# Output projection with channels on the partitions, its layer norm by products of ones, and c_fc_2 as a product of TensorE

## The chip, the cores and the metric

The kernel runs on one core of one Trainium2 chip. The metric is the device time of one execution in microseconds. The document speaks of the engines by the names that the profile gives them: PE (TensorE, the matrix products), PEld (its weight loads), DVE (VectorE), ACT (ScalarE), POOL (GpSimd), and SP, whose queue issues nearly all DMAs.

## The reference

Two layers work on an input of 4 batches, 384 channels and 32 x 32 positions. Layer 0 is a selective scan in four directions followed by a mixture of four experts; layer 1 is attention followed by a feed-forward part whose two weights are Kronecker products. The change touches only the end of layer 1, cut here to what matters:

```python
out = jnp.einsum('bhnm,bhmd->bhnd', attn, w)             # attention, 8 heads of 64
out = jnp.einsum('bne,ce->bnc', out, w_out) + b_out      # projection out, 512 -> 384
x = x + out                                              # residual
t = _to_tokens(x)
h = _ln_t(t) @ jnp.kron(c_fc_1, c_fc_2).T                # c_fc_1 (1536, 32), c_fc_2 (1, 12)
t = t + jax.nn.gelu(h, approximate=False) @ jnp.kron(c_proj_1, c_proj_2).T
x = _from_tokens(t, x)
```

`_ln_t` subtracts the mean over the 384 channels and divides by the root of the variance plus 1e-5. Because c_fc_2 has one row of 12, a token's 384 channels are first folded into 32 numbers (12 channels each, weighted by c_fc_2), called z below, and only these 32 go through c_fc_1.

## The kernel before, in words

A batch has 1,024 positions, worked on as two halves of 512 (`halves(i)`) or eight tiles of 128 (`MB`). The 384 channels are three chunks of 128 (`DC`).

The program has two strands. The scan strand (`scan_layer`) goes through batches 0 to 3 in turn. Its inner step, in `chunk`, multiplies on POOL (L438, and L466 for half of the tiles), makes decay factors on ACT (L447), scans and multiplies on DVE (L452, L459) and adds up on PE with a product of 512 columns (L473). There are 1,536 of these products, each shown as two PE instructions; one of them is called a row of the scan here. POOL's results lie in six buffers named bx, which the products of L473 free. The scan's loads (dtr, bcs) are issued by the SP queue.

The tail strand (`tail_batch`) does the rest of a batch: routing of its tokens to experts (`route`, whose DVE part is `places` and whose 16 scatters are issued by POOL at L681), the experts (L925, L940), their combination (L977), attention (L1026 to L1103) and `last_layers`. The tails of batches 0, 1 and 2 run beside the scan of later batches as far as they fit; routing of batch b+1 stands between the attention and the last layers of batch b. The tail of batch 3 comes after the whole scan.

No order is written out by hand. A scheduler merges the two strands into one fixed order of instructions for each engine while the program is built, by priorities and by its own estimate of times; on the chip each engine works through its own order, and an instruction that waits holds up those behind it. `last_layers` is issued with a raised priority. Tiles come from pools: a tile of tag "k4" takes any of 5 buffers for the batches 0 to 2 and of 4 for batch 3, and waits until the former user of a buffer is done. Attention weights (ex), the token tiles of routing and several small tiles of `last_layers` share this tag. Products in PSUM take one of 3 banks of tag "p" for batches 0 to 2, and of 6 for batch 3.

`last_layers` before the change, step by step:

- L1119 to L1123 load weights: wa and wb hold w_out (wb also c_fc_2 and b_out repeated over the partitions), wc the rest. L1129 scales a part of wc on DVE.
- L1135 loads the residual, one tile xt of 1.5 MB with tokens on the partitions. L1136 adds b_out to it on POOL.
- For each of the eight tiles of 128 tokens, L1142 makes the projection o_ps (tokens x 384 channels) from four pieces of attention output. DVE adds it to xt (L1145), multiplies the sum with c_fc_2 back into the bank (L1146) and adds up twelves into zt (L1147); `stats` takes mean and variance of each token (L541, L542).
- L1153 to L1157 finish the layer norm on the 32 numbers of z instead of on 384 channels and write them four times side by side; L1164 turns them by PE, and L1168 copies them out of PSUM.
- `hidden` makes the 1,536 hidden values of one half in two sets of six chunks: products (L1180), copies (L1186), one gelu over six (L1189), then f_acc (L1197).
- For each chunk of output channels L1207 multiplies with pj2 in four pieces, and L1211 adds xt turned by a product with the identity. ACT copies the result out (L1216), and SP stores it (L1217).

Of the kernel before, what the change touches and what calls it, by code (L numbers as in the profile page):

```python
# [17 lines left out]
P = 128  # L18
B = 4
D = 384  # L20
DC = D // P
HW = 32
L = HW * HW
HF = 512
NH = L // HF
# [26 lines left out]
MB = L // P  # L52
# [6 lines left out]
KR = 32  # L59
KJ = D // KR  # L60
# [7 lines left out]
    ("lnb", DC),  # L68
    ("pj2", KJ),
    ("c2", KJ),  # L70
]
COL = {}
_at = 0
# [37 lines left out]
def halves(i):  # L111
    return slice(i * HF, (i + 1) * HF)


class Body:
    def __init__(self, ctx, tc, a):
        self.tc, self.nc, self.a = tc, tc.nc, a
        nc = self.nc
        const = ctx.enter_context(tc.tile_pool(name="const", bufs=1))
        self.const = const  # L120


# [16 lines left out]
        self.c2sum = const.tile([P, 1], F32, tag="c2sum", name="c2sum")  # L139
        lo, hi = COL["c2"]  # L140
        nc.vector.tensor_reduce(self.c2sum, self.cols[:, lo:hi], AX.X, ALU.add)

    def exp_again(self, ins):

# [963 lines left out]
    def last_layers(self, b, att, room):  # L1108

        nc, a = self.nc, self.a
        nq = P // KR
        nt = INNER // P


        wa = room.tile([P, nt - 1, D], "kw", "wa")
        nc.sync.dma_start(out=wa, in_=a["wa"].rearrange("p (t d) -> p t d", d=D))  # L1119
        wb = room.tile([P, 3, D], "kw", "wb")  # L1120
        nc.sync.dma_start(out=wb, in_=a["wb"].rearrange("p (t d) -> p t d", d=D))
        wc = room.tile([P, 3, D], "kw", "wc")
        nc.sync.dma_start(out=wc, in_=a["wc"].rearrange("p (t d) -> p t d", d=D))  # L1123
        c2, bout = wb[:, 1, :], wb[:, 2, :]
        fc1 = wc[:, 0, :].rearrange("p (q m) -> p q m", m=P)
        pj1 = wc[:, 1, :].rearrange("p (f r) -> p f r", r=KR)
        pj2 = wc[:, 2, :]
        lo, hi = COL["pj2"]
        nc.vector.tensor_mul(  # L1129
            pj2.rearrange("p (r j) -> p r j", j=KJ), pj2.rearrange("p (r j) -> p r j", j=KJ),  # L1130
            self.cols[:, lo:hi].unsqueeze(1).to_broadcast([P, KR, KJ]),
        )

        xt = room.tile([P, MB, D], "k12", "xt")
        nc.sync.dma_start(out=xt, in_=self.tokens(b))  # L1135
        nc.gpsimd.tensor_add(xt, xt, bout.unsqueeze(1).to_broadcast([P, MB, D]))  # L1136
        zt = room.tile([P, MB, KR], "zt", "zt")
        for m in range(MB):
            ps = room.bank("p", "o_ps")[:, :D]
            for t in range(nt):  # L1140
                w = wa[:, t, :] if t < nt - 1 else wb[:, 0, :]
                nc.tensor.matmul(  # L1142
                    ps, att[t][:, m * P : (m + 1) * P], w, start=(t == 0), stop=(t == nt - 1)
                )
            nc.vector.tensor_add(xt[:, m, :], xt[:, m, :], ps)  # L1145
            nc.vector.tensor_mul(ps, xt[:, m, :], c2)  # L1146
            nc.vector.tensor_reduce(  # L1147
                zt[:, m, :], ps.rearrange("p (r j) -> p r j", j=KJ), AX.X, ALU.add
            )

        mean, rstd = self.stats(xt, self.eps5, room)
        shift = room.tile([P, MB], "shift", "shift")
        nc.vector.tensor_scalar(shift, mean, self.c2sum, None, op0=ALU.mult)  # L1153
        nc.vector.tensor_sub(zt, zt, shift.unsqueeze(2).to_broadcast([P, MB, KR]))
        z4 = room.tile([P, MB, nq, KR], "k4", "z4")
        for r in range(nq):
            nc.vector.tensor_mul(  # L1157
                z4[:, :, r, :], zt, rstd.unsqueeze(2).to_broadcast([P, MB, KR])
            )
        z = room.tile([P, L], "k4", "z")  # L1160
        for i in range(NH):
            ps = room.bank("p", "z_ps")
            for j in range(HF // P):
                nc.tensor.transpose(  # L1164
                    ps[:, j * P : (j + 1) * P],
                    z4[:, i * (HF // P) + j].rearrange("p r k -> p (r k)"), self.ident,
                )
            nc.vector.tensor_copy(z[:, halves(i)], ps)  # L1168


        ng = 6

        def hidden(i, at):
            hs = room.tile([P, ng, HF], "k12", "hs")
            early = None
            for f in range(at, at + ng, 2):
                banks = [room.bank("p", "h_ps") for _ in range(2)]
                for o, ps in enumerate(banks):
                    rows = slice((f + o) % nq * KR, ((f + o) % nq + 1) * KR)
                    ins = nc.tensor.matmul(  # L1180
                        ps, fc1[rows, (f + o) // nq, :], z[rows, halves(i)], start=True, stop=True
                    ).ins
                    if o == 0 and early is not None:
                        self.depend(ins, early)
                done = [
                    nc.scalar.copy(hs[:, f - at + o, :], ps).ins for o, ps in enumerate(banks)  # L1186
                ]
                early = done[0]
            self.exp_again(nc.scalar.activation(hs, hs, AF.Gelu).ins)  # L1189
            return hs  # L1190

        for i in range(NH):
            out = room.bank("o", "f_acc")
            for at in range(0, FC, ng):
                hs = hidden(i, at)
                for f in range(at, at + ng):
                    nc.tensor.matmul(  # L1197
                        out[f % nq * KR : (f % nq + 1) * KR, :], pj1[:, f, :], hs[:, f - at, :],
                        start=(f < nq), stop=(f >= FC - nq),
                    )  # L1200
            y = room.tile([P, HF], "k4", "fy")
            nc.vector.tensor_copy(y, out)
            for c in range(DC):
                ps = room.bank("p", "fo_ps")
                for j in range(HF // P):
                    cols = slice(j * P, (j + 1) * P)
                    nc.tensor.matmul(  # L1207
                        ps[:, cols], pj2[:, c * P : (c + 1) * P], y[:, cols],
                        start=True, stop=False,
                    )  # L1210
                    nc.tensor.matmul(  # L1211
                        ps[:, cols], xt[:, i * (HF // P) + j, c * P : (c + 1) * P], self.ident,
                        start=False, stop=True,
                    )
# [159 lines left out]
def layouts(inputs):  # L1374

    i = {k: np.asarray(v) for k, v in inputs.items()}

    def vec(v, lead):
        return np.moveaxis(v.reshape(*lead, P, -1), len(lead), 0).reshape(P, -1)
# [8 lines left out]
        "lnb": vec(i["L0_conv_ln_bias"], (DC,)),  # L1388
        "pj2": np.broadcast_to(i["L1_ffn_c_proj_2"].reshape(1, -1), (P, KJ)),
        "c2": np.broadcast_to(i["L1_ffn_c_fc_2"].reshape(1, -1), (P, KJ)),  # L1390
    }
# [3 lines left out]
    fc1 = i["L1_ffn_c_fc_1"].T  # L1395
    wx = np.zeros((D, KG // 2, XP), np.float32)
    wdt = np.zeros((KG, XP, D), np.float32)
    for k in range(KG):
# [19 lines left out]
        "wqkv": i["L1_conv_w_qkv"].T,  # L1418
        "wa": wout[:-1].transpose(1, 0, 2).reshape(P, -1),
        "wb": np.concatenate(  # L1420
            [
                wout[-1],
                np.broadcast_to(np.tile(i["L1_ffn_c_fc_2"].reshape(-1), KR), (P, D)),
                np.broadcast_to(i["L1_conv_b_out"], (P, D)),
            ],
            axis=1,
        ),
        "wc": np.concatenate(
# [25 lines left out]
```

## Time and profile before

| | |
|---|---|
| median of 3 runs | 4369.77 us (4367.19 to 4371.41) |
| the profiled execution | 4344.16 us |
| its span, from first to last instruction | 4342.4 us |
| mean granted clock of PE | 0.857 |
| busy: PE, DVE, ACT, POOL | 3303.7, 2915.6, 2504.3, 3049.3 us |
| last L438 of the scan begins | about 3480 us |
| o_ps (L1142) runs, batches 0 to 3 | about 1735 to 1780, 2745 to 2795, 3710 to 3780, 4232 to 4254 us |

The table of busy time counts how long an engine worked in a stretch; the list of waits says which instruction stood idle for which other one; a row of the groups gives line, engine, operation, output and inputs, shapes and count, then total busy time, the mean of one in ns, and the idle time before them with what ended it. The profiled execution is one execution of its own; it was 25 us shorter than the median of the three timed runs.

### The profile page before, as it was taken

To read this page: it belongs to the slowest core of one execution; us is meant where nothing else is said; L and a number is where in the kernel's file an instruction comes from. 1 tells how busy PE (TensorE), PEld (TensorE's weight loads), DVE (VectorE), ACT (ScalarE), POOL (GpSimd) and SP (SyncE) were. 2 spreads that over 40 slices of the span, in tenths; PEclk is the share of its full clock that TensorE was granted. 3 is DMA by queue.
4 is the path that set the end of the run, shared out by engine and by line. 5 is a ranking of instruction groups with operands and counts; after the bars stand their busy time and mean duration, and the time that the engine had idled before them with its cause. 6 is when DMAs were issued, how large, how long until landed. Compare 5 with 4: busy or idle time off the path is not lost. (4 is left out here: it accounts for less than half of the span.)

```text
span 4342.4 us, 45822 instructions
## 1 busy us (share of the span) xinstructions
PE 3303.7 (76%) x13340; PEld 1577.5 (36%) x13340; DVE 2915.6 (67%) x4331; ACT 2504.3 (58%) x4460; POOL 3049.3 (70%) x1475
## 2 busy tenths in 40 slices
PE   6444454398987885679986887569987889998896
PEld 2111111155552222245553222235554235666323
DVE  5999997887787868878886778967877730200101
ACT  5555555466665775467665776466665664343353
POOL 5999997798888968789998688778988820000100
PEclk8666666599998996789998999779998899999897
DMA  5444564567795535458888434457789443335200
GB/s 142 129 119 127 142 160 120 180 196 233 220 281 151 151 118 147 145 161 241 228 242 246 137 107 124 136 149 223 214 237 268 121 147 107 116 127 210 64 17 16
DMA packets 410131, 694.49 MB, mean 160 GB/s; under 512 B 50832, under 2 KB 209424, under 8 KB 409872
## 3 DMA queue, kind: packets, MB, share of 16 engines
q1 hardware_dynamic: 400560, 665.07, 53.6%
q0 software_dynamic: 8192, 25.17, 1.8%
q8 instruction: 107, 1.75, 0.2%
q14 instruction: 152, 1.25, 0.1%
q10 hardware_dynamic: 1120, 1.24, 0.1%
HBM read 569.79 MB, written 121.50 MB: 159 GB/s over the span
## 5 line engine op out<-in xcount | busy, mean ns | idle before, releaser
L438 POOL TENSOR_TENSOR bx<-dtr,bcs 128x1024 f32<-128x1024 f32 x768 | 1795.1, 2364 | 216.2 <-PE acc L473 103.2
L447 ACT ACTIVATE da<-dtr,nega 128x512 f32<-128x512 f32 x1536 | 1045.2, 690 | 994.2 <-DVE bx L459 628.9
L466 POOL TENSOR_TENSOR bx<-bx,bcs 128x1024 f32<-128x1024 f32 x384 | 905.2, 2362 | 160.3 <-DVE carry L463 67.3
L473 PE MATMUL acc<-bx,sel 128*32 128x512 f32 x3072 | 499.2, 702 | 342.4 <-POOL bx L466 273.7
L925 PE MATMUL h_ps<-xc,w 128*128 128x256 f32 (+1 forms) x3168 | 659.5, 363 | 52.0 <-DMA w<-in_w 27.0
L940 PE MATMUL y_ps<-w,hs 128*128 128x384 f32 x1824 | 649.6, 509 | 57.5 <-ACT hs L933 43.6
L925 PEld LDWEIGHTS h_ps<-xc,w 128*128 128x128 f32 x3168 | 547.6, 196 | 219.9 <-issue 92.3
L452 DVE TENSOR_TENSOR_SCAN bx<-da,carry,bx 128x512 f32<-128x512 f32 x384 | 474.0, 1269 | 140.4 <-POOL bx L438 79.5
L452 DVE TENSOR_TENSOR_SCAN bx<-da,bx 128x512 f32<-128x512 f32 x384 | 453.2, 1210 | 107.7 <-ACT da L447 61.7
L452 DVE TENSOR_TENSOR_SCAN da<-da,carry,bx 128x512 f32<-128x512 f32 x384 | 476.9, 1274 | 62.7 <-ACT da L447 51.8
L459 DVE TENSOR_TENSOR bx<-da,bcs 128x512 f32<-128x512 f32 x768 | 509.5, 679 | 3.1
L452 DVE TENSOR_TENSOR_SCAN da<-da,bx 128x512 f32<-128x512 f32 x384 | 455.7, 1219 | 76.0 <-ACT da L447 54.9
L940 PEld LDWEIGHTS y_ps<-w,hs 128*128 128x128 f32 x1824 | 353.6, 198 | 346.0 <-issue 75.7
L1055 ACT ACTIVATE ex<-s_ps 128x512 f32<-128x512 f32 x512 | 300.1, 590 | 157.1 <-PE s_ps L1049 156.1
L1049 PE MATMUL s_ps<-w 64*128 64x512 f32 x1024 | 309.9, 666 | 54.5 <-ACT ex L1055 53.8
L1095 PE MATMUL o_acc<-ex,vt 128*64 128x512 f32 x1024 | 285.6, 637 | 32.9 <-ACT ex L1055 23.5
L473 PEld LDWEIGHTS acc<-bx,sel 128*32 128x32 f32 x3072 | 77.0, 116 | 640.9 <-POOL bx L466 386.6
L930 ACT ACTIVATE hs<-h_ps,bb 128x256 f32<-128x256 f32 (+1 forms) x528 | 199.9, 439 | 185.3 <-PE h_ps L925 180.6
L961 POOL TENSOR_TENSOR diag<-ident,g_weight 128x1024 f32<-128x1024 f32 x8 | 15.1, 1899 | 326.9 <-DMA w<-in_w 312.1
L944 DVE TENSOR_TENSOR y<-y_ps,bb 128x384 f32<-128x384 f32 x76 | 41.7, 549 | 259.0 <-PE y_ps L940 259.0
L363 PE MATMUL dt_ps<-xd,wdt 108*128 108x512 f32 x192 | 123.9, 732 | 73.3 <-ACT mag L402 43.9
L1049 PEld LDWEIGHTS s_ps<-w 64*128 64x128 f32 x1024 | 83.5, 192 | 254.2 <-ACT ex L1055 202.3
(214 smaller groups left out, 3688.4 us busy)
## 6 DMA issues: line engine op xcount, KB each, us to landing
w<-in_w SPq DMA_DIRECT2D x352, 576.0 KB
dtr<-dd SPq DMA_DIRECT2D x1536, 128.0 KB
bcs<-both SPq DMA_DIRECT2D x512, 128.0 KB
dd<-one_e SPq DMA_DIRECT2D x96, 256.0 KB
dd<-mag SPq DMA_DIRECT2D x96, 256.0 KB
rows<-zero SPq DMA_DIRECT2D x76, 192.0 KB
xs<-rows SPq DMA_DIRECT2D x32, 384.0 KB
made<-y SPq DMA_DIRECT2D x32, 384.0 KB
```

The costliest lines, as they stand in the source:

```text
L438: pool = nc.gpsimd.tensor_mul(bx, dtr[q][1], bc[:, 0].unsqueeze(1).to_broadcast([P, 2, HF])).ins
L447: nc.scalar.activation(da, dtr[q][0][:, j, :], AF.Exp, scale=nega[:, col : col + 1])
L452: nc.vector.tensor_tensor_scan(run(h), run(da), run(bx[:, j, :]), 0.0 if first else hold, ALU.mult, ALU.add,)
L459: dve = nc.vector.tensor_mul(bx[:, j, :], h, cg).ins
L466: pool = nc.gpsimd.tensor_mul(bx, bx, cg.unsqueeze(1).to_broadcast([P, 2, HF])).ins
L473: nc.tensor.matmul(acc[lo : lo + DB, :], sel, out[q][:, j, :], start=(g == 0), stop=(g == NG - 1),)
L925: nc.tensor.matmul(ps[:, r, :], w1[(f + r) // wf][:, c, (f + r) % wf * P : ((f + r) % wf + 1) * P], xc[:, c, :], start=(c == 0), stop=(c = ...
L930: nc.scalar.activation(hs[:, f + r, :], ps[:, r, :], AF.Identity, bias=bb[:, f + r : f + r + 1])
L940: nc.tensor.matmul(out[:, :D], hs[:, f, t * P : (t + 1) * P], w2[f // wf][:, f % wf, :], start=(f == 0), stop=(f == FC - 1),)
L1049: ins = nc.tensor.matmul(ps, w[rows, j * P : (j + 1) * P], w[rows, halves(i)], start=True, stop=True).ins
L1055: done.append(nc.scalar.activation(ex[:, o, :], ps, AF.Exp, scale=HD**-0.5, accum_out=sums[:, t, 2 * j + o, i : i + 1],).ins)
L1095: ins = nc.tensor.matmul(out[cols, :], made[t][1][:, j, cols], ex[:, o, :], start=(j == 0), stop=(j == MB - 1),).ins
```

## The change

The projection is now made with channels on the partitions. For each half, three chunks of o_ps take four pieces of attention output, 512 columns wide; the residual is added in the same bank by products of its token tiles with the identity. It comes in four loads of two token tiles each (tag k4) in place of one. ACT evicts each chunk with b_out as a bias into x2 (channels x positions). Mean and variance come from products with a matrix of ones, as the earlier layer norms of this kernel do it; the centred values and their squares are needed only for the variance. z is a product of x2 with a matrix wz that holds c_fc_2, less its mean over the 384 channels (so that the mean of a token drops out); DVE subtracts that mean from wz once per batch. The inverse root is two activations over 512 columns, and z is its product with zp. At the output, one product of 512 columns stands for the four pieces, and DVE adds x2 while it copies out of PSUM, where ACT had copied. The rest of `last_layers` and all other functions are as they were; c2sum becomes c2mean.

```diff
-        wb = room.tile([P, 3, D], "kw", "wb")
+        wb = room.tile([P, 2, D], "kw", "wb")
...
-        c2, bout = wb[:, 1, :], wb[:, 2, :]
+        wz = wb[:, 1, :]
+        nc.vector.tensor_scalar(wz, wz, self.c2mean, None, op0=ALU.subtract)
...
-        xt = room.tile([P, MB, D], "k12", "xt")
-        nc.sync.dma_start(out=xt, in_=self.tokens(b))
-        nc.gpsimd.tensor_add(xt, xt, bout.unsqueeze(1).to_broadcast([P, MB, D]))
-        zt = room.tile([P, MB, KR], "zt", "zt")
-        for m in range(MB):
-            ps = room.bank("p", "o_ps")[:, :D]
-            for t in range(nt):
-                w = wa[:, t, :] if t < nt - 1 else wb[:, 0, :]
+        x2 = room.tile([P, DC, L], "k12", "x2")
+        zs = []
+        for i in range(NH):
+            part = []
+            for m in range(i * (HF // P), (i + 1) * (HF // P), 2):
+                part.append(room.tile([P, 2, D], "k4", "xt"))
+                nc.sync.dma_start(out=part[-1], in_=self.tokens(b)[:, m : m + 2, :])
+            for c in range(DC):
+                ps = room.bank("p", "o_ps")
+                chunk = slice(c * P, (c + 1) * P)
+                for t in range(nt):
+                    w = wa[:, t, chunk] if t < nt - 1 else wb[:, 0, chunk]
+                    nc.tensor.matmul(ps, w, att[t][:, halves(i)], start=(t == 0), stop=False)
+                for j in range(HF // P):
+                    nc.tensor.matmul(
+                        ps[:, j * P : (j + 1) * P], part[j // 2][:, j % 2, chunk], self.ident,
+                        start=False, stop=(j == HF // P - 1),
+                    )
+                nc.scalar.activation(
+                    x2[:, c, halves(i)], ps, AF.Identity, bias=self.col("bout", c)
+                )
+            mean = room.bank("p", "x2_mean")
+            for c in range(DC):
                 nc.tensor.matmul(
-                    ps, att[t][:, m * P : (m + 1) * P], w, start=(t == 0), stop=(t == nt - 1)
+                    mean, self.ones, x2[:, c, halves(i)], start=(c == 0), stop=(c == DC - 1)
                 )
-            nc.vector.tensor_add(xt[:, m, :], xt[:, m, :], ps)
-            nc.vector.tensor_mul(ps, xt[:, m, :], c2)
-            nc.vector.tensor_reduce(
-                zt[:, m, :], ps.rearrange("p (r j) -> p r j", j=KJ), AX.X, ALU.add
-            )
-
-        mean, rstd = self.stats(xt, self.eps5, room)
...
+            sq = room.tile([P, DC, HF], "k12", "x2_sq")
+            for c in range(DC):
+                nc.vector.scalar_tensor_tensor(
+                    sq[:, c, :], mean, -1.0 / D, x2[:, c, halves(i)], op0=ALU.mult, op1=ALU.add
                 )
-            nc.vector.tensor_copy(z[:, halves(i)], ps)
+                nc.scalar.activation(sq[:, c, :], sq[:, c, :], AF.Square)
+            zp = room.bank("p", "z_ps")
+            for c in range(DC):
+                nc.tensor.matmul(
+                    zp, wz[:, c * P : (c + 1) * P], x2[:, c, halves(i)],
+                    start=(c == 0), stop=(c == DC - 1),
+                )
+            var = room.bank("p", "x2_var")
+            for c in range(DC):
+                nc.tensor.matmul(var, self.ones, sq[:, c, :], start=(c == 0), stop=(c == DC - 1))
+            z = room.tile([P, HF], "k4", "z")
+            self.inverse_root(z, var, self.eps5, scale=1.0 / D)
+            nc.vector.tensor_mul(z, z, zp)
+            zs.append(z)
...
-                for j in range(HF // P):
-                    cols = slice(j * P, (j + 1) * P)
-                    nc.tensor.matmul(
-                        ps[:, cols], pj2[:, c * P : (c + 1) * P], y[:, cols],
-                        start=True, stop=False,
-                    )
-                    nc.tensor.matmul(
-                        ps[:, cols], xt[:, i * (HF // P) + j, c * P : (c + 1) * P], self.ident,
-                        start=False, stop=True,
-                    )
+                nc.tensor.matmul(ps, pj2[:, c * P : (c + 1) * P], y, start=True, stop=True)
                 o = room.tile([P, HF], "k4", "out")
-                nc.scalar.copy(o, ps)
+                nc.vector.tensor_add(o, ps, x2[:, c, halves(i)])
```

The weights that the host lays out follow: wb holds wz in place of the repeated c_fc_2 and b_out, and b_out joins the small columns.

More of the change, by code (lines that the diff above doesn't have):

```diff
@@ L70 @@
     ("c2", KJ),
+    ("bout", DC),
 ]
@@ L137, in __init__ @@
         nc.gpsimd.memset(self.minus1, -1.0)
-        self.c2sum = const.tile([P, 1], F32, tag="c2sum", name="c2sum")
+        self.c2mean = const.tile([P, 1], F32, tag="c2mean", name="c2mean")
         lo, hi = COL["c2"]
-        nc.vector.tensor_reduce(self.c2sum, self.cols[:, lo:hi], AX.X, ALU.add)
+        nc.vector.tensor_reduce(self.c2mean, self.cols[:, lo:hi], AX.X, ALU.add)
+        nc.vector.tensor_scalar_mul(self.c2mean, self.c2mean, 1.0 / D)
     def exp_again(self, ins):
@@ L1152, in last_layers @@
[L1152 to L1158, printed above, removed]
-            )
-        z = room.tile([P, L], "k4", "z")
-        for i in range(NH):
-            ps = room.bank("p", "z_ps")
-            for j in range(HF // P):
-                nc.tensor.transpose(
-                    ps[:, j * P : (j + 1) * P],
-                    z4[:, i * (HF // P) + j].rearrange("p r k -> p (r k)"), self.ident,
-                )
-            nc.vector.tensor_copy(z[:, halves(i)], ps)
+            sq = room.tile([P, DC, HF], "k12", "x2_sq")
@@ L1180, in hidden @@
                     ins = nc.tensor.matmul(
-                        ps, fc1[rows, (f + o) // nq, :], z[rows, halves(i)], start=True, stop=True
+                        ps, fc1[rows, (f + o) // nq, :], zs[i][rows, :], start=True, stop=True
                     ).ins
@@ L1204, in last_layers @@
                 ps = room.bank("p", "fo_ps")
-                for j in range(HF // P):
-                    cols = slice(j * P, (j + 1) * P)
-                    nc.tensor.matmul(
-                        ps[:, cols], pj2[:, c * P : (c + 1) * P], y[:, cols],
-                        start=True, stop=False,
-                    )
-                    nc.tensor.matmul(
-                        ps[:, cols], xt[:, i * (HF // P) + j, c * P : (c + 1) * P], self.ident,
-                        start=False, stop=True,
-                    )
+                nc.tensor.matmul(ps, pj2[:, c * P : (c + 1) * P], y, start=True, stop=True)
                 o = room.tile([P, HF], "k4", "out")
-                nc.scalar.copy(o, ps)
+                nc.vector.tensor_add(o, ps, x2[:, c, halves(i)])
                 nc.sync.dma_start(out=a["out"][b][c * P : (c + 1) * P, halves(i)], in_=o)
@@ L1390, in layouts @@
         "c2": np.broadcast_to(i["L1_ffn_c_fc_2"].reshape(1, -1), (P, KJ)),
+        "bout": vec(i["L1_conv_b_out"], (DC,)),
     }
@@ L1395, in layouts @@
     fc1 = i["L1_ffn_c_fc_1"].T
+    wz = np.zeros((KR, KJ, KR), np.float32)
+    wz[np.arange(KR), :, np.arange(KR)] = i["L1_ffn_c_fc_2"].reshape(1, -1)
+    wz = wz.reshape(D, KR)
     wx = np.zeros((D, KG // 2, XP), np.float32)
@@ L1420, in layouts @@
         "wb": np.concatenate(
[L1421 to L1425, printed above, removed]
+            [wout[-1], np.tile(wz, (1, nq)).reshape(DC, P, P).transpose(1, 0, 2).reshape(P, -1)],
             axis=1,
```

## The prediction

> **What bounds the kernel now.** I read the busy table by stretch first, with one stretch for each regime, then the waits, then single rows.
>
> ```profile
> core 0: us, PE busy (x) PEld busy (x) DVE busy (x) ACT busy (x) POOL busy (x), PEclk, DMA share, GB/s
> 100.00:600.00 500.00, 245.08 (x764) 60.68 (x758) 460.48 (x609) 266.92 (x417) 496.12 (x216) 0.66 0.52 132
> 1700.00:1800.00 100.00, 52.25 (x169) 24.11 (x169) 95.34 (x206) 41.43 (x71) 67.21 (x32) 0.69 0.34 100
> 2690.00:2800.00 110.00, 60.52 (x190) 25.59 (x188) 107.63 (x181) 44.23 (x75) 78.97 (x36) 0.73 0.33 95
> 3600.00:3900.00 300.00, 298.51 (x1260) 184.05 (x1259) 38.12 (x82) 127.05 (x218) 6.68 (x1) 1.00 0.37 120
> 4228.00:4342.00 114.00, 72.58 (x308) 37.21 (x306) 23.28 (x57) 40.07 (x49) 0.00 (x0) 0.72 0.04 15
> ```
>
> Four regimes. The scan alone (100 to 600) is bound by POOL, busy 496 of 500. Where the last layers of batches 0 and 1 run beside it (1700, 2690), DVE is full (95 of 100, 107.6 of 110) and POOL loses a third. Batch 2's last layers lie after the scan, among batch 3's experts, where PE is full (298.5 of 300). Batch 3's stand alone in the last 114 us, where nothing is full and the chain decides. Who waits in the second regime (1700 to 1800):
>
> ```profile
> ACT da L447 <- DVE bx L459: 31.2, 10, 7.9
> ACT da L447 <- DVE bx L452: 18.4, 10, 4.9
> POOL bx L438 <- PE acc L473: 14.9, 2, 8.7
> PE z_ps L1164 <- DVE z L1157: 12.5, 1, 12.5
> ```
>
> The scan waits for DVE. What DVE does there for the last layers, and its POOL partner:
>
> ```profile
> L1146 DVE TENSOR_TENSOR o_ps<-xt,wb 128x384 f32<-128x384 f32 x32 | 28.6, 893 | 0.4
> L1136 POOL TENSOR_TENSOR xt<-xt,wb 128x3072 f32<-128x3072 f32 x4 | 26.8, 6704 | 206.7 <-DMA wb<-in_wb 206.7
> L1026 PE MATMUL w_ps<-xc,wqkv 128*128 128x512 f32 x192 | 94.5, 640 | 1.7 <-ACT xc L1005 1.7
> L166 DVE SCALAR_TENSOR_TENSOR u<-ln_mean,u 128x512 f32<-128x512 f32 x24 | 15.0, 681 | 8.3 <-PE ln_mean L164 8.3
> ```
>
> L1146 reads two SBUF tiles. By stretch its eight take 9.44 us (batch 0), 10.17 (1), 4.53 (2) and 4.42 (3): double where POOL runs.
>
> **What the Trainium skill says.** "SBUF — State Buffer", section "SBUF: two separate sides": a DVE operation with two SBUF inputs and a GpSimd operation exclude each other for a whole instruction. The trace agrees (1.2 against 0.55 us for one L1146). All new DVE work but one small subtraction reads a PSUM tile, like L166, and should keep its 0.68. "TensorE: Matmul & The Clock Gate", "What's actually happening": idle about 3.4 us halves the array's clock. The trace agrees: a pair of L1211 after an idle stretch shows 0.63 us, later 0.39. "Perfetto Trace Analysis", "Identifying the Most-Contended Engine": matmul busy time alone doesn't prove that PE binds. So I took the waits of PE between 3600 and 3900: none is longer than 0.6 us.
>
> **The change by parts, per batch.** PE, at the full clock: a 512-column instruction costs 0.446 (the chain shows 12 of L1026 in 5.35), a 384-column one 0.335 (L1142, 20 in 6.66), a 128-column one of L1207 or L1211 0.111 (two start 0.22 apart). Before: 64 x 0.335 = 21.4 for o_ps, about 1.0 for the z transposes, 96 x 0.111 = 10.7 at the output: 33.1. After: 48 x 0.446 = 21.4 for o_ps, 48 x 0.111 = 5.3 for the residual by identity, 12 x 0.446 = 5.35 each for mean, z, variance and output: 48.1. So +15.0.
> DVE: removed are L1145, L1146, L1147, statistics, shift, z and its copies: 31.8 us in batch 0 and 27.7 in batch 1 (stretch sums). Added: 6 subtractions, 6 residual additions and 2 products at 0.68 = 9.5, and wz at 0.6. So -21.7 and -17.4. The wz subtraction may be held up as L1129 was once (11.8 us in batch 1, else 0.5 to 0.9): 0 to 11.
> ACT: 6 output copies (3.5) and 0.5 go; 6 biased evictions (no such row; between the copy's 0.59 and L367's 0.68), 6 squares at 0.62 and 2 x (0.655 + 0.580) come: +6, hidden, as ACT is 41 of 100 busy there.
> POOL: 6.7 of L1136 goes. In batch 0 (at 1603) POOL had waited 21 us for L473 around it, in batch 3 it stood alone; worth 0 to 6.7, taken as 0.
> DMA: wb shrinks by 192 KB; one 1.5 MB load becomes four of 384 KB, out of k4 buffers.
>
> **Batch 3, the chain.** Before: from the first bc_ps (4230.6) to the first h_ps (4264.3) 33.7. After, PE in its new order: 9 bc (0.6), 18 wa products (8.0), three chunks' wb and residual (5.3), bc, means and z (6.0), wait for the squares (0.6) and variance (0.9), the second half's o_ps 10.7, residual 2.7, variance 1.8, mean and z 5.3, waits 1.5: 43.4, so +9.7, since both halves now stand before the first h_ps. The first FFN half then starts on a warm clock (26.8, as the second half before, against 29.1): -2.3. The output products of each half take 4.4 at first half clock, against 7.8 and 8.3 (with the last copy): -3.3 and -3.0. Sum +1. The four xt loads wait for the last ex tiles; they have the 8.0 of wa products as cover.
> **Batch 2.** PE is full, so +15, and nothing of DVE's or POOL's gain counts. From both sides: 0 if idle PE later (3950 to 4050) takes it up, 20 if the two halves' waits for ACT and DVE aren't filled.
> **Batches 0 and 1, beside the scan.** A row is one 512-column product of L473 (two instructions; 1,536 rows). The rebuilt order keeps rows and tail in step: batch 0's first h_ps stays at row 812, its end goes from row 848 to 852; batch 1's from 1264 to 1280; batch 2's combine (L977) from 1480 to 1492. A new wait enters: the second half's xt tiles take buffers of the next batch's routing, free only when its 16 scatters (L681, 1.27 us apart) are done. The SP queue holds loads of dtr behind those two, and PE holds L473 behind the residual product, so POOL's bx buffers wait.
> Batch 0: the place computation gets DVE almost for itself: count product at 1733, 10 us of small operations and 14 of scan, done 1759 (before about 1802). Scatters to 1780, load and landing 8 (estimate: L1135's quarter), residual, mean and z 9.5 on a slow clock: 1798 for the first h_ps at row 812 (before 1793). Then 40 rows at 2.0 (POOL's 1,795 + 905 + 185 us for 1,536 rows is 1.9) and 3: 1881, against 1888, whose stretch held the scatters. -7.
> Batch 1 likewise: h_ps at 2814 (2811), end 2897 (2901): a further -4, say -11 in all.
> The experts stretches of batches 1 and 2 carry 4 rows less each, worth 2.2 us a row (224 rows in 491 us) or nothing if PE decides; half of 17.6 is -8. After L977 of batch 2, 12 rows fewer stand before the scan's end, at 1.95 (56 rows in 109 us): -24. Against it, three more attention steps and one projection lie after the scan: +9 (4 s_ps and 6 o_acc at 0.54, 6 w_ps at 0.446, 16 bc_ps at 0.055).
> **Sum.** -11 - 8 - 24 + 9 + 15 + 1 = -18 us. The profiled execution took 4344.16 (span 4342.4, 2 us around it); it lies 25 below the median of 4369.77, so I apply the difference: 4352.
>
> **Rivals.** (1) Slower: PE stands behind the scatters. If the placing isn't done by 1759, every us goes to h_ps and, once the six bx buffers are full, to the scan. For it: this wait is new and in order on PE and SP; against it: before, the scatters cost POOL 20 us later anyway. It decides from 9 us a batch, when the 18 are gone; at 20 each, 4370 - 18 + 40 = 4392; typical 4382. (2) More gain: DVE's relief comes through whole, -39 in place of -11: 4324; for it, DVE's 95%; against it, the FFN stretches wait for ACT's gelu. (3) No difference: the row gain is lost because PE, at 404 of 450 from 2900 to 3350, decides there: half of -32 goes, and 4368 is left.
>
> **How the numbers follow.** Chances: forecast (4338 to 4361) 0.38, rival 2 0.20, rival 3 0.18, rival 1 0.24. 0.2% of this kernel is 8.7 us, about what its measurement can tell. So faster 0.58, same 0.18, slower 0.24. The range goes from rival 2 with wz free and batch 2's PE work hidden (4324 - 12) to rival 1 near its end, 4388. The forecast's own range is 4338 to 4361.
>
> **What would show it.** Right: DVE under 90% in the two last-layers stretches, the scan's last L473 some 40 us earlier than 3481, PE still full for batch 2 with 48 us of these products, first h_ps to end of batch 3 about 69 us, before 78. Wrong: PE idle for long before a residual product, released by an xt load or a scatter; L447 or L438 still waiting there; DVE held in wz; or a batch 2 in which PE has gaps.

## The result, and the profile after

The changed kernel takes 4336.6 us, median of 7 runs (4328.09 to 4351.62), beside 4365.42 for the kernel before in the same set (a set is the runs of several kernels that were taken together). The ratio is 0.9939 with a 95% interval of 0.9921 to 0.9957: about 27 us, or 0.6%, faster. Differences from the kernel before are worked out from such ratios; differences between two changed kernels of one set are those of their medians, where nothing else is said. The profiled execution of the changed kernel has a span of 4326.3 us, 16.1 below the span of the one before.

The busy table by stretch, changed kernel (columns as in the table of before; PEclk is the first of the last three numbers):

```profile
core 0: us, PE busy (x) PEld busy (x) DVE busy (x) ACT busy (x) POOL busy (x), PEclk, DMA share, GB/s
100.00:600.00 500.00, 245.54 (x764) 60.66 (x758) 460.64 (x609) 266.91 (x417) 496.61 (x216) 0.66 0.50 132
1700.00:1800.00 100.00, 70.02 (x235) 30.15 (x235) 73.56 (x170) 49.87 (x84) 79.80 (x47) 0.84 0.63 190
2690.00:2800.00 110.00, 68.47 (x218) 30.28 (x217) 85.62 (x151) 50.83 (x87) 84.77 (x49) 0.78 0.51 159
3600.00:3900.00 300.00, 298.44 (x1171) 174.67 (x1171) 25.36 (x46) 124.49 (x213) 0.00 (x0) 1.00 0.38 125
```

The scan alone and batch 2's stretch look as before: POOL 496.6 of 500, PE 298.4 of 300. In the two stretches of last layers beside the scan, DVE falls from 95.3 to 73.6 of 100 and from 107.6 to 85.6 of 110. POOL, which binds the scan where it runs alone, rises from 67.2 to 79.8 and from 79.0 to 84.8.

The waits between 1700 and 1800, changed kernel (in total, times, longest):

```profile
...
DVE x_sq L1165 <- PE x_mean L1160: 15.7, 1, 15.7
...
PEld o_ps L1149 <- issue: 12.3, 40, 1.6
ACT x L1155 <- PE o_ps L1151: 11.1, 1, 11.1
ACT da L449 <- DVE bx L461: 9.6, 6, 2.6
ACT da L449 <- DVE bx L454: 9.4, 7, 4.0
...
POOL bx L440 <- PE acc L475: 6.0, 1, 6.0
PEld o_ps L1151 <- DMA xt<-x: 5.7, 2, 3.0
...
PE o_ps L1151 <- DMA xt<-x: 4.6, 2, 2.5
```

The scan's two waits for DVE (L447 before, L449 now) fall from 49.6 to 19.0 us. Among the longest is now DVE waiting for PE. Batch 1 has the same wait (2690 to 2920):

```profile
DVE x_sq L1165 <- PE x_mean L1160: 18.6, 1, 18.6
```

Together DVE stands idle for 34 us at these two places, before the second half's mean subtraction, while PE makes that half's projection. The prediction has no such wait; the experiment on the order of the halves comes back to it. The last two lines of the list are the new wait for the residual's tiles, seen on the weight loads and on PE: it is there, and small.

What the new operations cost, groups of the changed kernel:

```profile
L1220 DVE TENSOR_TENSOR out<-fo_ps,x 128x512 f32<-128x512 f32 x24 | 16.3, 684 | 16.7 <-PE fo_ps L1218 16.7
L1155 ACT ACTIVATE x<-o_ps,cols 128x512 f32<-128x512 f32 x24 | 15.4, 687 | 68.4 <-PE o_ps L1151 68.3
L1165 DVE SCALAR_TENSOR_TENSOR x_sq<-x_mean,x 128x512 f32<-128x512 f32 x24 | 15.1, 684 | 63.5 <-PE x_mean L1160 62.6 <-issue 0.9
L1127 DVE TENSOR_SCALAR wb<-wb,c2mean 128x384 f32<-128x384 f32 x4 | 3.3, 818 | 1.1 <-DMA wb<-in_wb 1.1
```

The subtractions and residual additions take 0.684 us (0.68 was assumed), in every stretch alike, and the wz subtraction takes 0.41 us in three batches and 2.04 in batch 1, where it was thus held by 1.6 at most.

To see where the time went, I take five places that both kernels pass, from the traces: the first product of each batch's combine (L977 before, L979 after), the start of the scan's last product, and the end. Times in us; the last column is a second trace of the changed kernel, from another execution.

| place | before | after | difference | second trace |
|---|---|---|---|---|
| combine of batch 1 | 2359.6 | 2352.5 | -7.1 | -14 |
| combine of batch 2 | 3361.1 | 3363.3 | +2.2 | -5 |
| last row of the scan | 3492.8 | 3456.4 | -36.4 | -42 |
| combine of batch 3 | 4031.0 | 4014.3 | -16.7 | -14 |
| end of the span | 4342.4 | 4326.3 | -16.1 | -13.5 |

(The prediction gives 3481 for the scan's last row; that was misread by 11 us, the trace has 3492.8.)

The gain is made up to the end of the scan, 20 us of it is given back between there and batch 3's combine, and batch 3 is even. A single trace places such differences to some 10 us only. Four traces of programs that are alike up to the end of the scan (the changed kernel twice, the one with the new form in batches 0 and 1 alone, and the one with more PE work in batch 2) have its last row between 3450.6 and 3467.8. So the experiments below go by medians of many runs. The median of the kernel before was 4365, 4360, 4341 and 4337 us in the four sets of runs. Ratios are therefore taken within a set; where two sets have to be compared, the text says so.

### The profile page after: what moved, and what is told of

Its sections match the earlier page's. It is cut to its first block, busy times and chain, and to the rows that moved or that the text cites. A ratio compares the mean times of both kernels' runs of the same rounds, so it can differ in the third digit from the quotient of the medians.

```text
span 4326.3 us, 45583 instructions
## 1 busy us (share of the span) xinstructions
PE 3343.5 (77%) x13244; PEld 1557.7 (36%) x13244; DVE 2860.4 (66%) x4200; ACT 2517.2 (58%) x4484; POOL 3021.3 (70%) x1471
## 5 line engine op out<-in xcount | busy, mean ns | idle before, releaser
L449 ACT ACTIVATE da<-dtr,nega 128x512 f32<-128x512 f32 x1536 | 1045.1, 690 | 940.0 <-DVE bx L461 574.9
L927 PE MATMUL h_ps<-xc,w 128*128 128x256 f32 (+1 forms) x3168 | 664.8, 365 | 64.5 <-DMA w<-in_w 20.2
L927 PEld LDWEIGHTS h_ps<-xc,w 128*128 128x128 f32 x3168 | 549.9, 197 | 236.8 <-issue 95.0
L963 POOL TENSOR_TENSOR diag<-ident,g_weight 128x1024 f32<-128x1024 f32 x8 | 15.1, 1901 | 453.9 <-PE xc_ps L910 440.7
L1097 PE MATMUL o_acc<-ex,vt 128*64 128x512 f32 x1024 | 285.9, 633 | 20.0 <-ACT ex L1057 15.7
```

What stands on the lines that cost most here:

```text
L449: nc.scalar.activation(da, dtr[q][0][:, j, :], AF.Exp, scale=nega[:, col : col + 1])
L927: nc.tensor.matmul(ps[:, r, :], w1[(f + r) // wf][:, c, (f + r) % wf * P : ((f + r) % wf + 1) * P], xc[:, c, :], start=(c == 0), stop=(c = ...
L1097: ins = nc.tensor.matmul(out[cols, :], made[t][1][:, j, cols], ex[:, o, :], start=(j == 0), stop=(j == MB - 1),).ins
```

## The experiments

**The changed kernel once more,** with no edit, beside three of the kernels below.

> The changed kernel once more, beside the three others of this call, for a narrower interval and a second trace. Forecast's sum: 18 us below the kernel before, ratio 0.996; the run of the result: 0.994. Sum of its two halves as measured (new form in batches 0 and 1: 0.992; in batches 2 and 3: 1.002): 0.994.

4336.25 us beside 4359.8, ratio 0.9945 (0.9926 to 0.9965). It repeats the result, and is again a little faster than the forecast's sum. Its trace is the second one of the table above.

**The two halves of the change.** The new form in batches 0 and 1 alone, beside the scan, and then in batches 2 and 3 alone. `last_layers_old` is the old function, with its weights loaded beside the new ones.

```
-            self.last_layers(b, att, room)
+            (self.last_layers if b < 2 else self.last_layers_old)(b, att, room)    # second kernel: b >= 2
```

> The new form in batches 0 and 1 only, batches 2 and 3 as before; the order beside the scan is that of the changed kernel, row for row. Theory A (the forecast's sum: about -32 us earned up to the attention of batch 2, +15 lost where PE is full in batch 2, +1 in batch 3): 16 us faster than the changed kernel, that is about 43 us below the kernel before, ratio 0.990. Rival B (batch 2's extra PE work is hidden, the gain is -27 whole): within 4 us of the changed kernel, ratio 0.994.

> The mirror image: the old form in batches 0 and 1, the new one in batches 2 and 3; the order beside the scan is that of the kernel before. Theory A: 16 us slower than the kernel before, ratio 1.0037, with last L473-like row at the same time as before and the loss between 3600 and 3900. Rival B: within 4 us of the kernel before, ratio 1.000.

New form in 0 and 1: 4329.07 beside 4364.85, ratio 0.992 (0.9902 to 0.9938), -35 us. New form in 2 and 3: 4375.02, ratio 1.0021 (1.0011 to 1.0032), +9 us (5 to 14). Both signs are those of theory A, and the two add up to -26, the changed kernel's own result. By itself the first lies midway between what the two theories expected (0.990 and 0.994). It is the second that excludes rival B, in which the loss after the scan was hidden; at 9 us it is smaller than the 16 expected. A second reading of the same term, in one set, comes with the kernels that take each form where it pays: 14 us by the ratios, 17.8 by the medians.

**PE work in batch 2.**

```
+            for _ in range(7 if b == 2 else 1):
                 for c in range(DC):
                     nc.tensor.matmul(var, self.ones, sq[:, c, :], ...)
```

> The changed kernel with batch 2's six variance products done seven times (same result): 6 x 12 x 0.446 = 32.1 us more of TensorE in the stretch where it is full; the order beside the scan stays row for row. Theory A (every us of PE counts there): 32 us slower than the changed kernel, so that the +9 measured for the new form in batches 2 and 3 would mean that the 15.0 of its PE work were overcounted. Rival B (idle PE later takes up about half): 14 to 18 us slower. Rival C (hidden): within 5 us.

4364.94 us beside 4336.25 for the changed kernel in the same set (ratios to before 1.0007 and 0.9945): 28.7 us for 32.1 of PE, 0.9 us for each, give or take a third. The stretch stays as full as it was, in the kernel with the extra products:

```profile
3600.00:3900.00 300.00, 299.60 (x1124) 169.54 (x1123) 23.11 (x42) 106.72 (x195) 0.00 (x0) 1.00 0.34 109
```

Theory A holds: here PE's time is the kernel's time. Counted from start to start of each product in batch 2's stretch, the old form's products take 32.5 us of PE and the new form's 46.9, so that the 15.0 were not overcounted either (14.4).

**PE work beside the scan.** The same four times instead of once in batches 0 and 1 (`range(4 if b < 2 else 1)`).

> The changed kernel with the variance products of batches 0 and 1 done four times (same result): 3 x 12 x 0.446 = 16.1 us more of TensorE a batch at the full clock, about 20 at the clock granted there, beside the scan. The forecast costs PE work there at nothing but its delay of the chain: 0 to 10 us slower than the changed kernel. If PE decides there as in batch 2: 32 to 40 us slower.

4350.27 us, ratio 0.998 (0.9968 to 0.9991): 14 us slower than the changed kernel in the same set, for 32.2 us of PE work. That lies between what was expected of the two cases: this work costs 0.43 us for each us (0.15 to 0.75 by the two intervals). It is not free, as the forecast took it. But the order beside the scan is not that of the changed kernel: here batch 2's combine stands behind row 1508 and no longer 1492. The table after the experiments on DVE shows that the loss stands behind the scan, and not beside it.

**DVE work beside the scan.**

```
+                for _ in range(3 if b < 2 else 1):
                     nc.vector.scalar_tensor_tensor(sq[:, c, :], mean, -1.0 / D, x2[:, c, halves(i)], ...)
...
+                for _ in range(3 if b < 2 else 1):
                     nc.vector.tensor_add(o, ps, x2[:, c, halves(i)])
```

> The changed kernel with each of the six mean subtractions and each of the six output additions of batches 0 and 1 done three times (same result): 12 x 0.68 + 12 x 0.72 = 16.8 us of DVE work a batch given back, 33.6 in both, of the 39 that the change takes off DVE there. If DVE's relief is what the gain comes from (0.8 to 1 us of time for each us of DVE): 27 to 34 us slower than the changed kernel, about as slow as the kernel before or 5 us slower, ratio 1.000 to 1.002. If the order of the rows is what it comes from (this order puts 12 to 24 more scan rows ahead of batch 2's attention): no slower than the changed kernel, ratio 0.994 or below. If about half of DVE's work is hidden there: ratio 0.998.

4353.77 us, ratio 0.9974 (0.9964 to 0.9983), 13 to 17 us slower than the changed kernel (by ratio and by median; the two were measured in different sets). So 33.6 us of such DVE work cost about half of themselves. More scan rows ahead of batch 2's attention gave no gain of their own: this order puts batch 2's first attention scores behind row 1524, in place of 1500, and the kernel is slower.

**The old form's own DVE work.** Two edits of the kernel before, in batches 0 and 1 only. Neither computes what the kernel before does, as the second normalization's input differs; they are there to weigh one instruction. The first leaves the multiplication by c_fc_2 out, the second leaves out the residual in what is multiplied.

```
-            nc.vector.tensor_mul(ps, xt[:, m, :], c2)
+            if b >= 2:
+                nc.vector.tensor_mul(ps, xt[:, m, :], c2)
+            src = ps if b >= 2 else xt[:, m, :]      # the reduction reads src
```

> The kernel before with the multiplication by c_fc_2 (L1146) left out in batches 0 and 1: the reduction reads xt at once. That takes 9.4 + 10.2 = 19.6 us off DVE, of instructions that wait for POOL, and nothing off PE. If half of DVE's time beside the scan counts, as when 33.6 us were given back for 16 us: 9 to 10 us faster than the kernel before, ratio 0.998. If it counts whole: 20 us faster, ratio 0.9955. If DVE's time does not count, or the gain of the change comes from elsewhere (POOL's addition, order): ratio 0.9995 to 1.0005.

```
-            nc.vector.tensor_mul(ps, xt[:, m, :], c2)
+            nc.vector.tensor_mul(ps, ps if b < 2 else xt[:, m, :], c2)
```

> The kernel before with the multiplication by c_fc_2 kept in batches 0 and 1, but reading the product in PSUM in place of the sum in SBUF (the residual is left out of the second normalization's input there), so that it reads one SBUF tile and not two. By the trace of the kernel before, it then lasts 0.55 in place of about 1.2 us: 19.6 - 8.8 = 10.8 us less of DVE. If what counts is DVE's time by the half: 5 us faster than the kernel before, ratio 0.9988. By the whole: 11 us, 0.9975. If what counts is that an operation on two SBUF tiles and one of POOL exclude each other, and stand in each other's way twice: most of the gain of leaving the multiplication out (ratio 0.990) is there, 30 to 40 us, ratio 0.991 to 0.993.

Left out: 4298.92 us beside 4341.47, ratio 0.9903 (0.9882 to 0.9923), -42 us. Reading PSUM: 4319.04 beside 4336.81, ratio 0.996 (0.9945 to 0.9975), -17 us. The first was foreseen by no theory: 19.6 us of DVE are worth 42 (33 to 51 by the interval), twice themselves. The second lies between two: 10.7 us are worth 17 (11 to 24), so that one for one is just possible and one half is not. The groups of the batch 0 stretch (1690 to 1900), first in the kernel before:

```profile
L1142 PE MATMUL o_ps<-wa,att 128*128 128x384 f32 x48 | 21.3, 589 | 6.8 <-DVE zt L1147 6.8
L1146 DVE TENSOR_TENSOR o_ps<-xt,wb 128x384 f32<-128x384 f32 x8 | 9.4, 1180 | 0.0
```

with the multiplication reading PSUM:

```profile
L1142 PE MATMUL o_ps<-wa,att 128*128 128x384 f32 x48 | 19.4, 544 | 4.8 <-DVE zt L1147 4.8
L1146 DVE TENSOR_TENSOR o_ps<-o_ps,wb 128x384 f32<-128x384 f32 x8 | 4.5, 557 | 0.0
```

and without it:

```profile
L1142 PE MATMUL o_ps<-wa,att 128*128 128x384 f32 x48 | 17.3, 496 | 1.8 <-DVE carry L463 1.0 <-DVE xt L1145 0.8
```

The same eight multiplications take 4.5 in place of 9.4 us once they read one SBUF tile: the other half was POOL's. The Trainium skill states that exclusion of DVE and GpSimd ("SBUF — State Buffer", section "SBUF: two separate sides"), and this trace agrees: with POOL idle, in batches 2 and 3, the multiplication of two SBUF tiles takes 0.56 us too.

The first line of each fence shows a second thing. The projection needs a bank of PSUM that DVE frees with the reduction L1147, so PE idles for it (6.8, 4.8 and then 1.8 us, none of the last for the reduction). The scan's products stand behind in PE's order: in the kernel before, POOL waits for them for 14.9 us between 1700 and 1800, as the prediction's list shows. So a microsecond of DVE can count a second time there.

A third part is the order of the rows, which the scheduler builds anew for each kernel. Its share shows when the traces are split at the end of the scan. Times in us; the last column is the time from the scan's last row to batch 3's combine.

| kernel | row before batch 2's combine | last row of the scan | from there to the combine of batch 3 |
|---|---|---|---|
| without the multiplication | 1468 | 3469.7 | 523.1 |
| multiplication reading PSUM | 1476 | 3474.5 | 534.5 |
| before | 1480 | 3492.8 | 538.2 |
| new form in 0 and 1 | 1492 | 3467.8 | 551.4 |
| new form in 2 and 3 | 1480 | 3504.0 | 559.2 |
| changed kernel, two traces | 1492 | 3456.4, 3450.6 | 557.9, 566.3 |
| residual's tiles in other buffers (next experiment) | 1488 | 3467.4 | 567.7 |
| PE work beside the scan | 1508 | 3457.7 | 583.9 |
| DVE work beside the scan | 1512 | 3465.7 | 590.7 |

The first four have the old form behind the scan, the last five the new one. (The kernels with another order of the halves, further down, stand before the combine at row 1492 too and take 1 to 17 us less behind the scan.) In both groups the stretch behind the scan grows with the rows that stand before batch 2's combine, by about 1.2 us a row in the first and 1.0 in the second (estimates: 28.3 us for 24 rows and 31.5 for 32). The more rows stand before it, the more of batch 2's tail is left when the scan ends, and there PE is full. So the two kernels with extra work in batches 0 and 1 end the scan within the scatter of the changed kernel, and lose behind it, where their code is that of the changed kernel. And of the 38 us by which the span of the kernel without the multiplication is shorter, 23 are there at the end of the scan and 15 come after it. The prices of PE and DVE work are therefore those of the work with the order that is built for it; no run holds the order fixed while it adds such work. How the 23 us divide between POOL's exclusion and the bank that PE waits for stays open.

**The residual's tiles in other buffers.**

```
-                part.append(room.tile([P, 2, D], "k4", "xt"))
+                part.append(room.tile([P, 2, D], "kw", "xt"))
```

> The changed kernel with the residual's xt tiles in the buffers of the weights (kw) in place of those that the routing's scatters hold (k4). The trace of the changed kernel shows PE idle for 10.3 us in batch 0 and 6.4 us in batch 1 before the residual products, for xt loads. If that wait costs the end (rival 1 in a small size): 8 to 17 us faster than the changed kernel, ratio 0.990 to 0.992. If PE's idle time there is covered by the scan's own waits (forecast): within 5 us of the changed kernel, ratio 0.993 to 0.995.

4352.11 us, ratio 0.9973 (0.9963 to 0.9984): 12 to 16 us slower than the changed kernel, by ratio and by median of two sets; neither theory had that. What PE and its weight loads wait for at the residual products (in us, times), in the changed kernel in batch 0 and in batch 1:

```profile
  DMA xt<-x: 10.3, 4
...
  DMA xt<-x: 6.4, 2
```

and in this one, in the same order:

```profile
  DMA xt<-x: 14.1, 4
...
  DMA xt<-x: 0.6, 2
```

These lines add up the wait of PE and that of its weight loads, which are the same idle time seen twice. PE alone stands idle for 4.6 us in batch 0 and 3.1 in batch 1 in the changed kernel, and for 6.5 and 0.2 here. The 10.3 and 6.4 us of the expectation, and the 8 to 17 us to be gained, were thus about twice too large from the start. The wait goes away in batch 1 and stays in batch 0. There the issue of the load waits for earlier residual products of PE in both kernels (up to 9.3 and 9.5 us in the SP queue), and not for the scatters. The tiles now take four of the eight buffers that weights stream through; whether that is what costs the 12 to 16 us was not shown, as PE's waits for weights are no longer in its trace than in that of the changed kernel (15.1 against 20.2 us at L927). This stays open; the order of the rows differs as well, by 4 before batch 2's combine.

**The order of the halves.** The changed kernel writes both halves' projections and normalizations, and then both halves' feed-forward stages. Here each half is finished first:

```
         for i in range(NH):
             part = []
             ...                      # projection, mean, variance, z of half i, as before
             zs.append(z)
-        for i in range(NH):
             out = room.bank("o", "f_acc")
             ...                      # feed-forward and output of half i
```

> The changed kernel with each half's feed-forward stage written ahead of the other half's projection. By the trace the first h_ps of batch 3 would start some 20 us earlier (10.7 projection, 2.7 residual, 5.3 mean and z, 1.8 variance), and the second half's PE work would fill PE's idle time under the gelu (5 to 6 us at each of two gelus). Forecast's chain: 8 to 12 us faster than the changed kernel in batch 3. Rival (the second half's x2_sq and the hs tiles share two buffers, so that the halves still stand one after the other): 0 to 5 us.

4315.57 us, ratio 0.9901 (0.9879 to 0.9923): 21 us faster than the changed kernel in the same set, but not where it was expected. In the trace batch 3 takes 323 us from its combine to the end, where the thirteen other traces of this study, none with this order there, lie between 308 and 314. The halves stand one after the other, as the rival had it, and slower than that: TensorE in batch 3 of this kernel (start, duration),

```profile
4237.49 4.90 PE L1215 MATMUL fo_ps<-fy,wc 128*128 128x512 f32 x6 [0.85 <-DVE fy L1212]
4242.23 2.74 PE L1170 MATMUL o_ps<-att,wa 128*128 128x512 f32 x6
```

the second half's first projection product (L1170) comes after the first half's output (L1215). Beside the scan the order gains: the first h_ps of batch 1 starts at 2756.6,

```profile
L1148 PE MATMUL h_ps<-z,wc x48: 587/1054/1217, 2756.6 to 2856.6; 32*128 32x512 f32 x48
```

where the changed kernel has 2809.7, and batch 2's combine starts at 3332 in place of 3363 and 3356. What went is the wait of DVE for the second half's mean: 18.6 us in the changed kernel's batch 1 (14.0 and 16.8 us in batches 0 and 1 of its second trace), and in this kernel nothing in batch 0 and, in batch 1,

```profile
DVE x_sq L1186 <- PE x_mean L1181: 0.6, 1, 0.6
```

In the changed kernel's batch 1 POOL, too, stood idle for 12.8 us there, until PE came to the scan's products behind the projection. No run removes this wait alone, so that it is the source of the gain is likely, but not shown.

**Each form where it pays.** The halves' order in batches 0 and 1; batches 2 and 3 in the old form in one kernel, in the changed kernel's form in the other.

```
-            self.last_layers(b, att, room)
+            (self.last_layers_halves if b < 2 else self.last_layers_old)(b, att, room)   # second kernel: else self.last_layers
```

> Batches 0 and 1 in the new form with each half's feed-forward stage ahead of the other half's projection, batches 2 and 3 as in the kernel before. If the three terms add up (21 us gained by the halves over the changed kernel, 11 more since batch 3 does not pay the 323 in place of 312 us from its combine to the end, 7 to 14 us for the old form in batch 2): 39 to 46 us below the changed kernel, ratio 0.984 to 0.986 to the kernel before. If batch 2's PE work is not what the new form costs after the scan: 32 below, ratio 0.987.

> The same, but batches 2 and 3 in the new form as the changed kernel has it. If the halves' gain lies beside the scan (batch 1's feed-forward starts at 2757 in place of 2803 in the traces) and batch 3 only loses by them: 32 us below the changed kernel, ratio 0.987. If batch 3 does not lose by them, or batch 2 gained: 15 to 21 below, ratio 0.990.

With the old form: 4287.87 us beside 4341.47, ratio 0.9886 (0.9864 to 0.9909), -49 us. With the new: 4305.66, ratio 0.9918 (0.9895 to 0.994), -36. In microseconds both lie within 2 us of what was expected (4290 to 4297 and 4304, from the changed kernel's 4336); as ratios they miss, since the kernel before was itself 20 us faster in this set than in those of the changed kernel. So the first beats the kernel before by a margin that is shown, while its margin over the changed kernel rests on a comparison of two sets (0.9886 against 0.9939 and 0.9945). What does not depend on that is the difference between the two, in one set and with the same order beside the scan: 17.8 us by the medians and 14 by the ratios for the new form in batches 2 and 3, where the forecast has 16. That batch 3 does not pay for the halves here is shown by the trace of the second kernel, 313 us from combine to end.

## Why the prediction was right, and where its steps were not

The forecast was -18 us, 4352; the profiled executions differ by 16.1 in span, the medians by 24 and 29 in two sets. 4336.6 lies within the range, but 1.4 us below the forecast's own (4338 to 4361), on the side of rival 2. Stage by stage the direction was right: a gain beside the scan, a loss behind it. That the sum came out near is in part luck, as two terms erred against each other. Point by point:

- **DVE's relief is visible and reaches the scan.** Right: DVE under 90% in both stretches (73.6 and 77.8), the scan's waits for it more than halved, and the last row 36 us earlier, against 40 announced.
- **Batch 0, -7.** Right in size: -7.1 at the next common place, batch 1's combine, 1.4 of which were there at batch 0's already. Its parts erred both ways. The scatters were done at 1773, not 1780, and the first h_ps came at 1786.2, not 1798; the 40 rows that followed took 99 us and not 83, so that the last output product ended at 1885 (1881 forecast).
- **Batch 1 and the experts' stretches, -4 and -8, then -24 for the 12 rows.** Here a step failed. At batch 2's combine the trace is at +2.2, where these steps put it at -19, and after it come -38.6 in place of -24. The first h_ps came on time (2809.7 against 2814), but the 40 rows up to the end took 96 us and not 83 (2905.9 against 2897). The step took 16 rows as done ahead of batch 1's end at next to no cost, and then took full credit for the rows saved after the combine. The sum at the scan's end was nearly right, -36.4 for -43, as the rows are the same ones: paid earlier, saved later.
- **The order, +9.** Of the right size: the kernel with the old form behind the scan and the changed kernel's order loses 13.2 us there by its trace (551.4 against 538.2).
- **PE work in batches 0 and 1 at nothing.** Wrong: the repeated products cost 0.43 us for each us of PE, order included, so that 2 x 15 cost about 13 (an estimate, which takes the same price for all products). **DVE's share** was too low by about as much: with -35 measured for the new form in these batches, all the rest must come to about -48 for 39 us of DVE, more than rival 2's full -39. The runs make this plausible and do not prove it: 33.6 us of DVE work put back cost only half of themselves, but those which the change takes away were partly held by POOL and freed banks that PE waits for, where 10.7 us were worth 17 and 19.6 worth 42, order included. The net of the forecast (-11 - 8 - 24 + 9 = -34) agrees with -35 because these two errors cancel.
- **DVE's wait for the second half's mean.** Missing from the prediction: 15.7 and 18.6 us in batches 0 and 1. It asked what PE would wait for, and took DVE as relieved.
- **Batch 2, +15.** Right: 14.4 more by the start-to-start count, at 0.9 us of time for each, so 13; both forms of batches 2 and 3 compared give 9 (5 to 14) in one set and 14 to 18 in another, for 16 forecast.
- **Batch 3, +1.** Right: 312.0 us from combine to end, 311.4 before; from the first h_ps (4256.3) to the end 70.0, where 69 were announced and 78.1 stood before.
- **The new wait (rival 1).** Present but not deciding: PE idles for 4.6 us in batch 0 and 3.1 in batch 1 before residual products, and in batch 0 not for the reason given. Rival 3 is excluded by the interval. Rival 2 (4324) is nearer to the measured median than it looked: 4336.6 lies about midway between it and the forecast.

## What to carry to other kernels

A microsecond has no price of its own: in this kernel it was worth 0.43 on TensorE beside the scan and 0.9 where TensorE is full, 0.5 on VectorE for operations that read PSUM, and 1.6 to 2.1 for operations which read two SBUF tiles beside a busy GpSimd and free a bank that TensorE needs. So before moving work from one engine to another, ask of each instruction who shares its port and who waits for its buffer; here, making one multiplication read PSUM was worth two thirds of the whole change, in a kernel which leaves the residual out of it.

Where a scheduler builds the order, such a price holds for the work and the new order together. So look in the trace where the loss stands before putting it down to an engine: here it stood behind the scan, though the work was added beside it.

A rewrite which trades one engine for another should be taken only in the stages where the engine it relieves is the one that binds. And ask which engine will wait for the one that got the work.

## What the runs showed of the hardware

- The 128x384 multiplication of two SBUF tiles took 1.18 and 1.27 us on average beside GpSimd's products (batches 0 and 1), 0.56 where GpSimd was idle (batches 2 and 3), and 0.56 beside GpSimd once one operand was in PSUM. Ten of the sixteen beside GpSimd were held (1.04 to 2.54 us each). Each of the ten ended 0.42 to 0.43 us after the GpSimd instruction that ran when it started.
- GpSimd paid too, but little: eight of its 1,152 products of the scan in the kernel before took over 2.55 us (the median is 2.36), all beside the last layers of batches 0 and 1. With the multiplication reading PSUM none did.
- In the stretch 1700 to 1800 TensorE was busy for 52.3 us in the kernel before and 70.0 in the changed one, and its granted clock was 0.69 and 0.84. Whether the clock pays for a part of the added products, no run isolates.
- The same kernel's median differed by 28 us (4337 to 4365) between sets of runs, as much as the change itself. Effects of this size are settled by comparisons within a set.
